# Norm factors by a power on GpSimd, a second norm from the first's statistics, and sigmoids as tanh, in a four-layer kernel on one core

## The chip, the cores and the metric

The chip is a Trainium2. The kernel runs on one of its cores, with that core's five engines: TensorE (PE; its weight loads are listed apart as PEld), VectorE (DVE), ScalarE (ACT), GpSimd (POOL) and SyncE (SP). Each engine works through its own queue of instructions in order, and waits on semaphores for the others. The metric is the device time of one launch in microseconds; the figure quoted for a kernel is the median of its runs.

## The reference, cut to what matters

Four batches of 1024 tokens with 128 features in float32, pass through four layers. Every layer has the same frame: a normalisation over the features, and then the sum of the input, an attention branch and a feed-forward branch, both fed with the normalised input.

```python
xn = _layernorm(x, axis=-1)          # (x - m) / sqrt(v + 1e-5), no gain, no bias
x = x + attn_l(xn, ...) + ffn_l(xn, ...)
```

Layer 0 has a memory attention and a mixture of eight experts, of which each token takes two. Layer 1 has a linear attention and a gated feed-forward with dequantised weights. Layer 2 is the one that the change touches most. Its attention branch normalises `xn` a second time, mixes neighbouring tokens by a convolution of width 3, and runs a gated recurrence over the tokens:

```python
h = (x - mu) * rsqrt(var + eps) * ln_g + ln_b       # x here is xn: a norm of a norm
mixed = conv_width_3(h) + mix_b
u, x_state = tanh(mixed @ Wi + bi), tanh(mixed @ Wsin + bsin)
decay, select = sigmoid(mixed @ Wd + bd), sigmoid(mixed @ Wsel + bsel)
state = decay * state + (1 - decay) * x_state       # scan over the tokens
y = (select * states) @ Wso + bso
g = sigmoid(mixed @ Wg + bg)
return x + (g * y + (1 - g) * u) @ Wout + bout
```

Layer 3 has an attention by phases (cosines and sines of learned angles), with a normalisation of what it retrieves, and a gated feed-forward in a 4-bit format.

## The kernel before, in words

The tokens of a batch lie on the 128 partitions in NT = 8 tiles of 128 features; B = 4 batches. `x[b]` (the running sum) and `xn[b]` (its norm) are 128x1024 tiles that stay in SBUF, and `xnT[b]` is `xn[b]` transposed, features on the partitions, with a zero column at either end.

`layernorm` (L198 to L213) takes one batch: eight `bn_stats` (L203) and eight `bn_aggr` (L205) on VectorE give mean and variance of the eight tiles as columns of `ln_mv`; ScalarE takes the square root of variance plus epsilon, eight columns at once (L207); VectorE takes its reciprocal (L208) and then does eight times subtract-and-multiply, 128x128 each (L210). ScalarE evaluates its functions from tables, and where the next function is in none that is loaded, an instruction ACT_TABLE_LOAD stands ahead of it, which the profile lists under the line of that function.

`prologue` (L230) runs `layernorm` from `x[b]` to `xn[b]` for its batches, and then `to_features` (L215), which transposes on TensorE (L220) and copies from PSUM on ScalarE (L223, or L225 with gain and bias). `add_psum` (L240) adds a PSUM result to half a batch of `x` on VectorE. `add_row` (L242) runs on GpSimd: it adds `xn` to `x` where asked (L245) and a row of biases to it (L246), each 128x1024.

The order of the stages is that of the Python; the order of instructions within each engine's queue is fixed when the kernel is built, by a scheduler that ranks what is ready, so work of later batches and of the next stage is interleaved with what goes before. At run time nothing overtakes. Queues that matter here are GpSimd's, VectorE's and ScalarE's.

Layer 0 ends with the experts: GpSimd scatters normalised tokens into lists by 64 indirect DMAs (L399), and the experts' results are gathered back by 64 more (L636), sixteen for each batch, in `combine` (L630), which layer 1 calls one batch ahead: the loop of layer 1 runs, for each batch, `attention(b)` (L648), the first half of `ffn`, `combine(b + 1)` and `prologue([b + 1])`, the second half of `ffn`, and `add_row`. The gathers have 24 buffers.

Layer 2 (L715 to L771) calls `prologue()` for all batches, then for each batch `layernorm(xn[b], hn)`, `add_row`, `to_features` into `hT` and the convolution on VectorE into `mixT` (L728 to L731). Then three projections of all batches into 128 partitions (32 states of 4 batches) give `xs`, `dec` and `sel` (L744), `drive`, and one scan of 1024 steps. In the loop over eight half batches after it, `u`, `g` and `y` are formed (L757 to L766) and projected into `po2`. `ffn` with Silu (L257) closes it.

Layer 3 (L775 to L945) calls `prologue()` and `add_row` for all batches, forms gates, and then goes batch by batch through the phases: sums in PSUM, products with cosines and sines on VectorE, GpSimd's running sums `run` (L887) and `rsum` (L894), `layernorm(bld, bld)` in place (L898), and the 4-bit feed-forward with Silu (L926), whose dequantised products `xq` and `hh` GpSimd forms (L294).

Of the kernel before, what the change touches and what calls it, by code (L numbers as in the profile page):

```python
# [10 lines left out]
F32 = mybir.dt.float32  # L11
I32 = mybir.dt.int32
AF = mybir.ActivationFunctionType
ALU = mybir.AluOpType
AX = mybir.AxisListType

P = 128
D = 128
B = 4
L = 1024  # L20
NT = L // P
NTT = B * NT
TB = 512
# [13 lines left out]
LN_EPS = 1e-5  # L37
# [32 lines left out]
def _cut(t, cols):  # L70
    out, at = {}, 0
    for name, n in cols:
        out[name] = t[:, at : at + n]
        at += n
    return out
# [3 lines left out]
def decoder4_kernel(  # L79
# [21 lines left out]
    V, S, G, T = nc.vector, nc.scalar, nc.gpsimd, nc.tensor  # L101

    const = ctx.enter_context(tc.tile_pool(name="const", bufs=1))
    state = ctx.enter_context(tc.tile_pool(name="state", bufs=1))
    small = ctx.enter_context(tc.tile_pool(name="small", bufs=2))
# [12 lines left out]
    def ps(name="ps"):  # L118
        n_ps[0] += 1
        return psum.tile([P, 512], F32, tag="ps", name=f"{name}_{n_ps[0]}")  # L120

    def pf(name):
        n_ps[0] += 1
        return psum.tile([P, 512], F32, tag="pf", name=f"{name}_{n_ps[0]}")


    x = []
# [28 lines left out]
    eps_c = const.tile([P, 1], F32, tag="eps", name="eps_c")  # L156
# [9 lines left out]
    W2 = _cut(w2_sb, W2_COLS)  # L166
# [19 lines left out]
    xn = [state.tile([P, NT, D], F32, tag=f"xn{b}", name=f"xn{b}") for b in range(B)]  # L186

    xnT = [state.tile([P, L + 2], F32, tag=f"xnT{b}", name=f"xnT{b}") for b in range(B)]
# [4 lines left out]
    def blk(t, i):  # L193

        c = 1 + (i % 2) * TB
        return t[i // 2][:, c : c + TB]

    def layernorm(src, dst):  # L198

        st = small.tile([P, NT, 6], F32, tag="ln_st", name="ln_st")  # L200
        mv = small.tile([P, NT, 2], F32, tag="ln_mv", name="ln_mv")
        for j in range(NT):
            V.bn_stats(st[:, j, :], src[:, j, :])  # L203
        for j in range(NT):
            V.bn_aggr(mv[:, j, :], st[:, j, :])  # L205
        rstd = small.tile([P, NT], F32, tag="ln_rstd", name="ln_rstd")
        S.activation(rstd, mv[:, :, 1], AF.Sqrt, bias=eps_c)  # L207
        V.reciprocal(rstd, rstd)  # L208
        for j in range(NT):
            V.tensor_scalar(  # L210
                dst[:, j, :], src[:, j, :], mv[:, j, 0:1], rstd[:, j : j + 1],
                ALU.subtract, ALU.mult,
            )  # L213

    def to_features(src, dst, g=None, bias=None):  # L215

        for h in range(2):
            pt = ps("pt")
            for j in range(4):
                T.transpose(pt[:, j * P : (j + 1) * P], src[:, 4 * h + j, :], ident)  # L220
            cols = dst[:, 1 + h * TB : 1 + (h + 1) * TB]
            if g is None:
                S.copy(cols, pt)  # L223
            else:
                S.activation(cols, pt, AF.Identity, bias=bias, scale=g)  # L225

    def mm(o, lhsT, rhs, start=True, stop=True):
        T.matmul(o, lhsT, rhs, start=start, stop=stop)  # L228

    def prologue(batches=range(B)):  # L230
        for b in batches:
            layernorm(x[b], xn[b])
        for b in batches:
            to_features(xn[b], xnT[b])

    def add_psum(i, p):

        h = (i % 2) * 4
        xv = x[i // 2][:, h : h + 4, :].rearrange("p j d -> p (j d)")
        V.tensor_tensor(xv, p, xv, ALU.add)  # L240

    def add_row(b, row, also=None):  # L242

        if also is not None:
            G.tensor_tensor(x[b], x[b], also, ALU.add)  # L245
        G.tensor_tensor(x[b], x[b], row.unsqueeze(1).to_broadcast([P, NT, D]), ALU.add)  # L246

    def ffn(guf, dnf, pool, blocks=range(NBLK)):
        for i in blocks:
            xT = blk(xnT, i)  # L250
            hid = pool.tile([P, NHC, TB], F32, tag="ffn_hid", name="ffn_hid")
            for c in range(NHC):
                pg, pu = pf("pg"), pf("pu")
                mm(pg, guf[:, 0, c, :], xT)
                mm(pu, guf[:, 1, c, :], xT)
                sg = pool.tile([P, TB], F32, tag="ffn_sg", name="ffn_sg")
                S.activation(sg, pg, AF.Silu)  # L257
                V.tensor_tensor(hid[:, c, :], sg, pu, ALU.mult)  # L258
            po = pf("po")
            for j in range(4):  # L260
                for c in range(NHC):
                    mm(po[:, j * D : (j + 1) * D], hid[:, c, j * P : (j + 1) * P], dnf[:, c, :],
                       c == 0, c == NHC - 1)
            add_psum(i, po)
# [36 lines left out]
    for t in range(NTT):  # L301
        b, j = divmod(t, NT)
# [3 lines left out]
    def l0t(tag, n=NS):  # L306
        return l0w.tile([P, n], F32, tag=tag, name=tag)
# [13 lines left out]
    for n in range(2):  # L321
        m = l0t(f"m{n}", NTT)
        V.tensor_reduce(m, by_e(sc), AX.X, ALU.max)
        w = l0t("w")
# [71 lines left out]
    for t in range(NTT):  # L396
        b, j = divmod(t, NT)
# [155 lines left out]
    xsT, hT, ex, hid, po = {}, {}, {}, {}, {}  # L553
# [159 lines left out]


    with tc.tile_pool(name="l2p", bufs=2) as l2p, tc.tile_pool(name="l2s", bufs=1) as l2s:  # L715
        prologue()
        hT, mixT = [], []
        for b in range(B):
            hn = l2p.tile([P, NT, D], F32, tag="hn", name="hn")
            layernorm(xn[b], hn)  # L720
            add_row(b, R["bout2"], xn[b])
            h = big.tile([P, L + 2], F32, tag="b1", name="hT")
            G.memset(h[:, 0:1], 0.0)
            G.memset(h[:, L + 1 : L + 2], 0.0)
            to_features(hn, h, g=W2["ln_g"], bias=W2["ln_b"])
            mx = big.tile([P, L + 2], F32, tag="b2", name="mixT")
            mv = mx[:, 1 : L + 1]
            V.tensor_scalar(mv, h[:, 1 : L + 1], W2["mix_w"][:, 1:2], W2["mix_b"],  # L728
                            ALU.mult, ALU.add)
            V.scalar_tensor_tensor(mv, h[:, 0:L], W2["mix_w"][:, 0:1], mv, ALU.mult, ALU.add)  # L730
            V.scalar_tensor_tensor(mv, h[:, 2 : L + 2], W2["mix_w"][:, 2:3], mv,  # L731
                                   ALU.mult, ALU.add)
            hT.append(h)
            mixT.append(mx)

        par = {}
        for nm, w, bias, fn in (("xs", "Wsin", "bsin", AF.Tanh), ("dec", "Wd", "bd", AF.Sigmoid),
                                ("sel", "Wsel", "bsel", AF.Sigmoid)):
            t = l2s.tile([P, L], F32, tag=nm, name=nm)
            for h in range(2):  # L740
                pst = ps("pst")
                for b in range(B):
                    mm(pst[b * SD : (b + 1) * SD, :], W2[w], blk(mixT, 2 * b + h))
                S.activation(t[:, h * TB : (h + 1) * TB], pst, fn, bias=W2[bias])  # L744
            par[nm] = t
        drive = l2s.tile([P, L], F32, tag="drive", name="drive")
        V.scalar_tensor_tensor(drive, par["dec"], 1.0, par["xs"], ALU.subtract, ALU.mult)
        states = l2s.tile([P, L], F32, tag="states", name="states")
        V.tensor_tensor_scan(states, par["dec"], drive, 0.0, ALU.mult, ALU.subtract)
        V.tensor_tensor(states, par["sel"], states, ALU.mult)  # L750
        for i in range(NBLK):
            b, h = divmod(i, 2)
            mT = blk(mixT, i)
            pu, pgg, py = ps("pu2"), ps("pgg"), ps("py")
            mm(pu, W2["Wi"], mT)
            u = l2p.tile([P, TB], F32, tag="u", name="u")
            S.activation(u, pu, AF.Tanh, bias=W2["bi"])  # L757
            mm(pgg, W2["Wg"], mT)
            g = l2p.tile([P, TB], F32, tag="g", name="g")
            S.activation(g, pgg, AF.Sigmoid, bias=W2["bg"])  # L760
            rb = slice(b * SD, (b + 1) * SD)
            mm(py, W2["Wso"][rb, :], states[rb, h * TB : (h + 1) * TB])
            y = l2p.tile([P, TB], F32, tag="y", name="y")
            V.scalar_tensor_tensor(y, py, W2["bso"], u, ALU.add, ALU.subtract)
            V.tensor_tensor(y, y, g, ALU.mult)
            V.tensor_tensor(y, y, u, ALU.add)  # L766
            po = pf("po2")
            for j in range(4):
                mm(po[:, j * D : (j + 1) * D], y[:, j * P : (j + 1) * P], W2["Wout"])
            add_psum(i, po)  # L770
        ffn(*ffn_w[1], l2p)  # L771
    l12.close()
# [2 lines left out]
    with tc.tile_pool(name="l3s", bufs=1) as l3s:  # L775
# [61 lines left out]
        with (  # L837
# [5 lines left out]
            for b in range(B):  # L843
# [16 lines left out]
                for j in range(NT):  # L860
                    t = b * NT + j
# [39 lines left out]
                for h in range(2):  # L901
                    po = ps("po3")
# [6 lines left out]
                for h in range(2):  # L909
# [26 lines left out]
                    po = pf("pof")  # L936
# [99 lines left out]
```

## Time and profile before

| what | value |
|---|---|
| time, median of 3 runs (lowest to highest) | 1124.07 us (1120.93 to 1126.26) |
| the profiled execution's own time | 1128.6 us |
| its span | 1126.8 us |
| TensorE clock granted, mean | 0.83 |
| busy, PE / PEld / DVE / ACT / POOL | 779.8 / 528.4 / 619.7 / 347.6 / 278.6 us |
| square roots on ScalarE, and table loads ahead of them | 24 of 300 ns, and 15 of 1283 ns |
| POOL's scatters (L399) and gathers (L636) | 64 of 1045 ns, 64 of 967 ns |

Times in the profile are microseconds from the start of the span. A row of a group gives engine and operation, output and input by name, shapes, the count, then busy time and the mean of one in ns, then how long the engine had been idle just before and what released it. A row of the timeline gives the start, the length, the engine, the line and the operation, and in brackets the idle time before it with its releaser; "issue" is a wait for nothing that the profile shows, and "remote" one for an event that it can't place. The profiled execution is one of its own and lies 4.5 us above the median.

### The profile page before, as it was taken

What the parts mean: (1) busy time and instruction counts of PE and PEld (TensorE: products, weight loads), DVE (VectorE), ACT (ScalarE), POOL (GpSimd) and SP (SyncE); (2) the same over time, 40 slices, a digit from 0 to 9 for tenths busy, and PEclk for the clock granted to TensorE, in tenths of its full rate; (3) what the DMA queues carried; (4) which work ended last, traced back from release to release, by engine and by line L of the source; (5) the groups of instructions that cost most, each with busy time, mean ns of one, the idle gap of its engine ahead of it and who ended that gap; (6) DMA issues with size and microseconds to landing.
All of it is one profiled execution on the core that took longest, in us unless ns stands there. A gap on an engine that the chain in (4) does not pass through costs nothing.

```text
span 1126.8 us, 10401 instructions
## 1 busy us (share of the span) xinstructions
PE 779.8 (69%) x3432; PEld 528.4 (47%) x3432; DVE 619.7 (55%) x1644; ACT 347.6 (31%) x551; POOL 278.6 (25%) x276
## 2 busy tenths in 40 slices
PE   2685156899991564695826999889967676667763
PEld 1543133566660243463612456555745555446652
DVE  6493023344443245659786546640187796796773
ACT  2041012233330252564624224421332314214121
POOL 2067720000005706112230003120032231341420
PEclk9988677999996777988957799967697797788867
DMA  9511100022211101000000000000000000000000
GB/s 341 160 36 49 52 23 16 29 76 68 73 55 51 54 6 37 10 10 1 1 1 0 1 1 1 1 0 1 1 0 1 10 10 10 10 0 10 10 3 16
DMA packets 44090, 34.73 MB, mean 31 GB/s; under 512 B 3334, under 2 KB 41030, under 8 KB 43782
## 3 DMA queue, kind: packets, MB, share of 16 engines
q1 hardware_dynamic: 39414, 23.61, 6.9%
q0 software_dynamic: 4624, 10.46, 3.0%
q8 instruction: 28, 0.46, 0.2%
q14 instruction: 24, 0.20, 0.1%
HBM read 18.40 MB, written 15.66 MB: 30 GB/s over the span
## 4 chain that ended last, share of the span: by engine, by line
PE 50%; DVE 22%; ACT 8%; another core or an unknown queue 7%; issue 6%; POOL 5%; DMA 1%; POOLq 0%; SPq 0%; ACTq 0%; DVEq 0%
PE ph L228 6%; PE po L228 5%; PE pg L228 4%; PE pu L228 4%; PE pm L228 3%; PE plg L228 3%; PE pt L220 3%; PE pmoe L228 3%; PE pgh L228 2%; PE pof L228 2%; DVE ln_st L203 2%; PE pth L934 1%; POOL rsum L894 1%; DVE xn L210 1%
## 5 line engine op out<-in xcount | busy, mean ns | idle before, releaser
L399 POOL DMA_INDIRECT xs_d<-xn,slot x64 | 66.9, 1045 | 71.9 <-DVE slot L382 52.7
L636 POOL DMA_INDIRECT yg<-ys_d,slot x64 | 61.9, 967 | 69.6 <-DVE x L699 50.4
L228 PE MATMUL ph<-w_sb,xsT 128*128 x142 | 74.8, 610 | 4.5 <-ACT xsT L566 4.4
L220 PE MATMUL pt<-ident,xn 128*128 128x128 f32 x128 | 30.4, 382 | 62.1 <-DVE xn L210 34.3
L228 PE MATMUL po<-dnf,ffn_hid 128*128 128x128 f32 x384 | 54.4, 290 | 22.2 <-DVE ffn_hid L258 22.2
L228 PEld LDWEIGHTS po<-dnf,ffn_hid 128*128 128x128 f32 x384 | 52.0, 205 | 34.5 <-DVE ffn_hid L258 29.2
L228 PE MATMUL pu<-xnT,guf 128*128 128x512 f32 x96 | 52.4, 628 | 11.8 <-ACT ffn_sg L257 11.8
L228 PE MATMUL pm<-val,tri 128*128 128x256 f32 x64 | 25.4, 484 | 48.7 <-DVE val L870 43.7
L585 DVE COPY moe_hT<-ph 128x256 f32<-128x256 f32 x71 | 30.2, 425 | 50.4 <-PE ph L583 50.4
L228 PE MATMUL pg<-xnT,guf 128*128 128x512 f32 x96 | 54.5, 652 | 3.2 <-ACT ffn_sg L257 3.2
L894 POOL TENSOR_TENSOR rsum<-ret 128x256 f32<-128x256 f32 x32 | 27.3, 854 | 111.0 <-DVE ret L892 106.3
L220 PEld LDWEIGHTS pt<-ident,xn 128*128 128x128 f32 x128 | 21.3, 176 | 68.8 <-issue 29.8
L934 PE MATMUL pth<-ident,hh 128*128 128x128 f32 (+1 forms) x96 | 22.5, 395 | 39.9 <-POOL hh L294 39.9
L240 DVE TENSOR_TENSOR x<-po,x 128x512 f32<-128x512 f32 x32 | 22.0, 688 | 50.3 <-PE po L228 37.1
L258 DVE TENSOR_TENSOR ffn_hid<-ffn_sg,pu 128x512 f32<-128x512 f32 x48 | 32.8, 683 | 30.0 <-PE pu L228 15.6
L576 ACT ACTIVATE moe_sg<-ph 128x256 f32<-128x256 f32 x71 | 27.3, 385 | 64.1 <-PE ph L228 64.1
L257 ACT ACTIVATE ffn_sg<-pg 128x512 f32<-128x512 f32 x48 | 28.7, 597 | 57.6 <-PE pg L228 57.4
L228 PE MATMUL pmoe<-w3e_sb,moe_hT 128*128 x284 | 43.5, 276 | 0.6 <-DVE moe_hT L585 0.5
L228 PEld LDWEIGHTS pmoe<-w3e_sb,moe_hT 128*128 128x128 f32 x284 | 38.6, 191 | 9.1 <-issue 8.1
L578 DVE TENSOR_TENSOR moe_hid<-moe_sg,ph 128x256 f32<-128x256 f32 x71 | 29.3, 413 | 24.7 <-ACT moe_sg L576 24.7
L245 POOL TENSOR_TENSOR x<-x,xn 128x1024 f32<-128x1024 f32 x8 | 18.9, 2364 | 95.9 <-DVE xn L210 95.9
L246 POOL TENSOR_TENSOR x<-x,rows_sb 128x1024 f32<-128x1024 f32 x12 | 29.3, 2442 | 44.0 <-DVE x L240 43.5
(351 smaller groups left out, 1922.7 us busy)
## 6 DMA issues: line engine op xcount, KB each, us to landing
xs_d<-zeros SPq DMA_DIRECT2D x18, 256.0 KB, 4.5
xs<-xs_d SPq DMA_DIRECT2D x17, 256.0 KB, 2.8
ys_d<-ys SPq DMA_DIRECT2D x17, 256.0 KB, 2.3
x<-in_x_in_dram SPq DMA_DIRECT2D x4, 512.0 KB, 12.0
w_sb<-in_w12T_dram SPq DMA_DIRECT2D x1, 2048.0 KB, 15.9
out_dram<-x SPq DMA_DIRECT2D x8, 256.0 KB, 2.3
w3e_sb<-in_w3T_dram SPq DMA_DIRECT2D x1, 1024.0 KB
xs_d<-xn,slot POOLq DMA_INDIRECT x64
```

The source lines that it names most:

```text
L220: T.transpose(pt[:, j * P : (j + 1) * P], src[:, 4 * h + j, :], ident)
L228: T.matmul(o, lhsT, rhs, start=start, stop=stop)
L246: G.tensor_tensor(x[b], x[b], row.unsqueeze(1).to_broadcast([P, NT, D]), ALU.add)
L257: S.activation(sg, pg, AF.Silu)
L258: V.tensor_tensor(hid[:, c, :], sg, pu, ALU.mult)
L399: G.indirect_dma_start(out=views[2 * t + n], out_offset=bass.IndirectOffsetOnAxis(ap=slots[n][:, t : t + 1], axis=0), in_=xn[b][:, j, :], ...
L576: S.activation(sg, ph[:, :HM], AF.Silu)
L578: V.tensor_tensor(hid[k], sg, ph[:, HM:], ALU.mult)
L585: V.tensor_copy(hT[k].rearrange("p c s -> p (c s)"), ph2[:, : 2 * P])
L636: G.indirect_dma_start(out=yg, out_offset=None, in_=ys_d, in_offset=bass.IndirectOffsetOnAxis(ap=slots[n][:, t : t + 1], axis=0),)
L894: G.tensor_tensor(rsum, ret[:, :, 0, :], ret[:, :, 1, :], ALU.add)
L934: T.transpose(pt[:n, j * P : (j + 1) * P], hh[:, j, o : o + n], ident)
```

## The change

It has three parts.

- The norm's factor: ScalarE's square root and VectorE's reciprocal are replaced by a multiply-and-add of eight columns on VectorE (variance plus epsilon) and a power of -1/2 on GpSimd (`rsqrt`). A constant tile `half_n` holds the exponent.
- In layer 2 the second norm is no longer measured. The first norm's output has mean 0, and its variance is known from the first's: rstd squared times the variance. `layernorm` gets an argument `again` for this; eight more multiplications, 128x128 each, write `hn`. The call of `prologue()` gives way to `layernorm` and `to_features` inside the loop over batches.
- In layer 2 the sigmoids become tanh of half the argument: sigmoid(z) = (tanh(z/2) + 1)/2. The halves go into biases (`hb`), into ScalarE's scale, and into scaled weights (`Wso4`, `Wout2`); `dec` needs one more multiply-and-add on VectorE, and three tensor-by-tensor instructions become ones that take a scalar too.

```diff
@@ -195,7 +195,16 @@
         c = 1 + (i % 2) * TB
         return t[i // 2][:, c : c + TB]
 
-    def layernorm(src, dst):
+    half_n = const.tile([P, NT], F32, tag="half_n", name="half_n")
+    G.memset(half_n, -0.5)
+
+    def rsqrt(dst, src, scale=1.0):
+
+        V.tensor_scalar(dst, src, scale, LN_EPS, ALU.mult, ALU.add)
+        G.tensor_tensor(dst, dst, half_n, ALU.pow)
+
+    def layernorm(src, dst, again=None):
+
 
         st = small.tile([P, NT, 6], F32, tag="ln_st", name="ln_st")
         mv = small.tile([P, NT, 2], F32, tag="ln_mv", name="ln_mv")
@@ -204,13 +213,19 @@
         for j in range(NT):
             V.bn_aggr(mv[:, j, :], st[:, j, :])
         rstd = small.tile([P, NT], F32, tag="ln_rstd", name="ln_rstd")
-        S.activation(rstd, mv[:, :, 1], AF.Sqrt, bias=eps_c)
-        V.reciprocal(rstd, rstd)
+        rsqrt(rstd, mv[:, :, 1])
         for j in range(NT):
             V.tensor_scalar(
                 dst[:, j, :], src[:, j, :], mv[:, j, 0:1], rstd[:, j : j + 1],
                 ALU.subtract, ALU.mult,
             )
+        if again is not None:
+            r2 = small.tile([P, NT], F32, tag="ln_r2", name="ln_r2")
+            V.tensor_tensor(r2, rstd, rstd, ALU.mult)
+            V.tensor_tensor(r2, r2, mv[:, :, 1], ALU.mult)
+            rsqrt(r2, r2)
+            for j in range(NT):
+                V.tensor_scalar(again[:, j, :], dst[:, j, :], r2[:, j : j + 1], None, ALU.mult)
 
     def to_features(src, dst, g=None, bias=None):
 
@@ -713,11 +728,19 @@
 
 
     with tc.tile_pool(name="l2p", bufs=2) as l2p, tc.tile_pool(name="l2s", bufs=1) as l2s:
-        prologue()
+
+        Wso4 = l2s.tile([P, D], F32, tag="Wso4", name="Wso4")
+        V.tensor_scalar(Wso4, W2["Wso"], 0.25, None, ALU.mult)
+        Wout2 = l2s.tile([P, D], F32, tag="Wout2", name="Wout2")
+        V.tensor_scalar(Wout2, W2["Wout"], 0.5, None, ALU.mult)
+        hb = l2s.tile([P, 3], F32, tag="hb", name="hb")
+        for n, nm in enumerate(("bd", "bsel", "bg")):
+            V.tensor_scalar(hb[:, n : n + 1], W2[nm], 0.5, None, ALU.mult)
         hT, mixT = [], []
         for b in range(B):
             hn = l2p.tile([P, NT, D], F32, tag="hn", name="hn")
-            layernorm(xn[b], hn)
+            layernorm(x[b], xn[b], hn)
+            to_features(xn[b], xnT[b])
             add_row(b, R["bout2"], xn[b])
             h = big.tile([P, L + 2], F32, tag="b1", name="hT")
             G.memset(h[:, 0:1], 0.0)
@@ -734,20 +757,22 @@
             mixT.append(mx)
 
         par = {}
-        for nm, w, bias, fn in (("xs", "Wsin", "bsin", AF.Tanh), ("dec", "Wd", "bd", AF.Sigmoid),
-                                ("sel", "Wsel", "bsel", AF.Sigmoid)):
+        for nm, w, bias, scale in (("xs", "Wsin", W2["bsin"], 1.0), ("dec", "Wd", hb[:, 0:1], 0.5),
+                                   ("sel", "Wsel", hb[:, 1:2], 0.5)):
             t = l2s.tile([P, L], F32, tag=nm, name=nm)
             for h in range(2):
                 pst = ps("pst")
                 for b in range(B):
                     mm(pst[b * SD : (b + 1) * SD, :], W2[w], blk(mixT, 2 * b + h))
-                S.activation(t[:, h * TB : (h + 1) * TB], pst, fn, bias=W2[bias])
+                S.activation(t[:, h * TB : (h + 1) * TB], pst, AF.Tanh, bias=bias, scale=scale)
             par[nm] = t
+
         drive = l2s.tile([P, L], F32, tag="drive", name="drive")
         V.scalar_tensor_tensor(drive, par["dec"], 1.0, par["xs"], ALU.subtract, ALU.mult)
+        V.tensor_scalar(par["dec"], par["dec"], 0.5, 0.5, ALU.mult, ALU.add)
         states = l2s.tile([P, L], F32, tag="states", name="states")
         V.tensor_tensor_scan(states, par["dec"], drive, 0.0, ALU.mult, ALU.subtract)
-        V.tensor_tensor(states, par["sel"], states, ALU.mult)
+        V.scalar_tensor_tensor(states, par["sel"], 1.0, states, ALU.add, ALU.mult)
         for i in range(NBLK):
             b, h = divmod(i, 2)
             mT = blk(mixT, i)
@@ -757,16 +782,17 @@
             S.activation(u, pu, AF.Tanh, bias=W2["bi"])
             mm(pgg, W2["Wg"], mT)
             g = l2p.tile([P, TB], F32, tag="g", name="g")
-            S.activation(g, pgg, AF.Sigmoid, bias=W2["bg"])
+            S.activation(g, pgg, AF.Tanh, bias=hb[:, 2:3], scale=0.5)
             rb = slice(b * SD, (b + 1) * SD)
-            mm(py, W2["Wso"][rb, :], states[rb, h * TB : (h + 1) * TB])
+            mm(py, Wso4[rb, :], states[rb, h * TB : (h + 1) * TB])
+
             y = l2p.tile([P, TB], F32, tag="y", name="y")
             V.scalar_tensor_tensor(y, py, W2["bso"], u, ALU.add, ALU.subtract)
-            V.tensor_tensor(y, y, g, ALU.mult)
-            V.tensor_tensor(y, y, u, ALU.add)
+            V.scalar_tensor_tensor(y, g, 1.0, y, ALU.add, ALU.mult)
+            V.scalar_tensor_tensor(y, u, 2.0, y, ALU.mult, ALU.add)
             po = pf("po2")
             for j in range(4):
-                mm(po[:, j * D : (j + 1) * D], y[:, j * P : (j + 1) * P], W2["Wout"])
+                mm(po[:, j * D : (j + 1) * D], y[:, j * P : (j + 1) * P], Wout2)
             add_psum(i, po)
         ffn(*ffn_w[1], l2p)
     l12.close()
```

## The prediction

> **What bounds the kernel now.** First the page: busy shares and the chain that ended last.
>
> ```profile
> PE 779.8 (69%) x3432; PEld 528.4 (47%) x3432; DVE 619.7 (55%) x1644; ACT 347.6 (31%) x551; POOL 278.6 (25%) x276
> PE 50%; DVE 22%; ACT 8%; another core or an unknown queue 7%; issue 6%; POOL 5%; DMA 1%; POOLq 0%; SPq 0%; ACTq 0%; DVEq 0%
> ```
>
> No engine bounds the whole, and ACT, which the change relieves most, holds 8% of the chain. So second, busy time by stretch (columns: stretch: length, then busy us and count of PE, PEld, DVE, ACT, POOL, then clock and DMA). I cut at the stages' ends: 345 to 446 is layer 1 while POOL gathers, 562 to 607 is layer 2's head, 607 to 664 its scan and mix, 812 to 1127 layer 3's batches.
>
> ```profile
> 345.00:446.00 101.00, 40.71 (x151) 26.10 (x151) 35.41 (x127) 24.20 (x35) 53.66 (x59) 0.70 0.13 37
> 562.00:607.00 45.00, 15.67 (x64) 8.55 (x63) 38.68 (x139) 11.46 (x19) 11.66 (x5) 0.58 0.00 1
> 607.00:664.00 57.00, 51.46 (x160) 22.21 (x160) 28.22 (x38) 20.43 (x28) 0.17 (x3) 0.85 0.00 0
> 812.00:1127.00 315.00, 207.39 (x974) 165.27 (x972) 228.86 (x491) 88.63 (x135) 87.19 (x69) 0.81 0.03 7
> ```
>
> Layer 2's head is VectorE's alone (38.7 of 45 us). From 607 PE rules; layer 3's batches are shared; in the gathers nobody is busy. Third, VectorE's groups inside 562 to 607:
>
> ```profile
> L210 DVE TENSOR_SCALAR hn<-xn,ln_mv,ln_rstd 128x128 f32<-128x128 f32 x32 | 12.1, 451 | 0.0
> L203 DVE BATCH_NORM_STATS2 ln_st<-xn 128x6 f32<-128x128 f32 x32 | 6.9, 273 | 0.0
> L205 DVE BATCH_NORM_AGGREGATE ln_mv<-ln_st 128x2 f32<-128x6 f32 x40 | 4.0, 155 | 0.0
> L208 DVE RECIPROCAL ln_rstd<-ln_rstd 128x8 f32<-128x8 f32 x5 | 0.9, 187 | 0.0
> ```
>
> The second norm's statistics, all 32 of them, stand here. Fourth, ACT's groups, whose last column says what the square roots and their loads wait for:
>
> ```profile
> L207 ACT ACT_TABLE_LOAD x15 | 19.2, 1283 | 7.2 <-DVE ln_mv L205 7.0
> L744 ACT ACT_TABLE_LOAD x2 | 2.6, 1283 | 4.8 <-PE pst L228 4.7
> L207 ACT ACTIVATE ln_rstd<-ln_mv,eps_c 128x8 f32<-128x8 f32 x24 | 7.0, 300 | 89.8 <-DVE ln_mv L205 65.1 <-DVE x L640 24.6
> ```
>
> ACT stood idle 89.8 us ahead of the square roots: it had loaded and was waiting. Most loads are therefore hidden. Fifth, POOL, since the power goes there: its timeline in the gathers, and two rows of its groups.
>
> ```profile
> 440.52 0.95 POOL L636 DMA_INDIRECT yg<-ys_d,slot  x1 [0.30 <-issue]
> 441.77 0.95 POOL L636 DMA_INDIRECT yg<-ys_d,slot  x1 [0.30 <-issue]
> ```
>
> ```profile
> L894 POOL TENSOR_TENSOR rsum<-ret 128x256 f32<-128x256 f32 x32 | 27.3, 854 | 111.0 <-DVE ret L892 106.3 <-DVE ln_mv L205 4.7
> L887 POOL TENSOR_TENSOR run<-run,val 128x512 f32<-128x512 f32 x20 | 26.6, 1328 | 28.0 <-DVE val L872 26.2 <-DVE ln_st L203 1.8
> ```
>
> Gathers follow each other every 1.25 us, in order; whatever is built behind them waits.
>
> **What the Trainium skill says.** "ScalarE: Activation LUTs", section "What ACT_TABLE_LOAD costs", gives about 1283 ns for a load and a drain behind it; the trace has 1283 ns for each and shows ACT's next activation starting at once (load at 1097.74, Silu at 1099.03), so I price a load at 1.28. "GPSIMD Engine Reference", sections 1 and 2.1: its SBUF port is shared with VectorE. The trace agrees: eight normalisations take 2.14 us alone, and 5.65 beside POOL's adds at 574.16. The same page, section 7, gives an fp32 dependent chain 4 cycles an element; no page prices a power.
>
> **The power's price.** The trace has none. Lower end, from the two POOL rows: (1328-854)/256 = 1.85 ns a column, so 380 ns at zero width and 0.4 us at 8 columns. Upper end: if it is a chain of 50 steps of 4 cycles at 1.2 GHz, 0.17 us a column, 1.3 us, plus 0.4: an estimate of 1.7 from that page; lane by lane it could be over 10. I take P = 0.6. It replaces a square root (0.30) and a reciprocal (0.20) by a VectorE scale-and-add (0.1) and the power, with two hand-overs as before: nothing at P = 0.4, +0.2 here, some 12 times on the path: two in layer 0, four in layer 1, two in layer 2, four in layer 3. That is +2.5 in all; it is within the stage sums below.
>
> **Part by part.** The build order of the changed kernel has 26 fewer table loads (33.4 us of ACT) and 24 fewer square roots (7.0 us).
>
> *Layer 0:* the first load is issued at 7.0 while x still lands (until 15.6), and VectorE has the statistics of other batches to do between a root and its use: 0 (-1 to +2; with a power of 2 us or more its cover is gone, and the excess counts twice).
>
> *Layer 1, a loss.* The powers stand in POOL's order after gathers 22, 55 and 64. Batch 0: square root at 368.35; gather 22 ends at 373.1, so +5. PE then runs into a stall it has anyway: from 377 to 404 it got 'remote' or 'issue' waits of 9 to 10 us, ending only when the gathers ended (395.7, last release 401.6). I take +2 (1 to 5.5). Batch 1: square root at 429.33, gather 55 ends at 441.5, +12; VectorE stands behind it, but its next instruction, the residual add L240, was released only at 445.30, as was ACT's qz. The transposes and xnT then finish after that instead of before, so pq is late by about 2.7 (1 to 6). Batch 2: square root 478.76, gather 64 ends at 482.63, normalisation at 479.44 becomes 483.3; the residual add waited for PE until 485.5, so pq at 485.30 slips to about 488: +3 (2 to 4). Batch 3 has no gathers: 0. Sum +7.5 (4 to 15).
>
> *Layer 2's head, the gain.* Now 44.0 us, from the end of layer 1's last residual add at 562.85 to that of the last mixT at 606.82. Removed on VectorE: 6.9 + 32 x 0.155 less overlap, 3.2, + 4 x 0.19 = 10.9 us. Added: two 8-column products and two scale-and-adds per batch, most before 562, about 0.8 in here; two 128x128 weight scalings and three tiny bias ones, 0.6. Batches 1 to 3 also lose waits between their second statistics and hn, but batch 3 gains a serial step: POOL's add L245 (2.35 us) sits ahead of its second power, so VectorE waits some 2 us where it now has mixT work to do. Normalisations beside POOL's adds are stretched either way (3.5 us now at 574). Net -9 (-12 to -5). The SP queue moves nowhere.
>
> *Sigmoids.* At L744 tanh stands between loads at 608 and 610.65: 2.6 us, with PE's products done and VectorE waiting for dec and sel, so on the path: -2.6; the new dec scale-and-add of 128x1024 (nearest row L728, 0.81 us, on a narrower mix of operands) lands between drive and scan: +0.7. Net -1.9. The y chain has the same three VectorE instructions.
>
> *Rest of layer 2 and layer 3's head (664 to 812).* PE is busy 66 of 71 and 73 of 77 us. Four Sqrt-Silu pairs go; each delayed a Silu by 1.3 to 2.6, of which PE noticed 0.3 to 1: -2.5 (-4 to -1).
>
> *Layer 3's batches.* Four Sqrt loads, all hidden (ACT idle 3.5 to 9.4 us before the root), and four Silu loads go (sine and Silu share a set in the build). The last, at 1097.74, delays Silu by about 0.4 as the product ends at 1098.6; the one at 866.40 by 1.3. The power in batch 1 waits behind hh on POOL (937.43, 2.59 us) but PE waited for that hh until 940.07. -2 (-5 to +3).
>
> Sum: 7.5 - 9 - 1.9 - 2.5 - 2 = -7.9, against the profiled execution, 1128.6 us (span 1126.8 and 1.8 around it): 1120.7. That one lies 4.5 above the median 1124.07, so the same step gives 1116.
>
> **Rivals.** Bound of what can be told: 0.5%, 5.6 us.
> *A, a dear power (slower).* The sum turns at P = 0.6 + 7.9/12 = 1.26 us, and is 0.5% slower from 1.7. At 3 us: -7.9 + 12 x 2.4 = +21, 1145. For it: a power is a long loop in software, unpriced. Against: 8 columns only. Chance 0.17.
> *B, the gathers' queue uncovered.* If PE's stalls move along with the late norms, layer 1 pays 5 + 12 + 4 = 21: 1129.6. For it: PE waited 27.6 us for that first root. Against: the stalls end with the gathers, which start no later. 0.13.
> *C, layer 1 absorbs it all* and VectorE's whole 12 us in the head count: 0 - 12 - 1.9 - 4 - 2 = -20, 1104. For it: the stall ends are POOL's. 0.17.
> *D, nothing seen*: the head's gain is given back by POOL's serial adds (5 us) and layer 1: 1122 to 1126. 0.08.
>
> **The numbers.** Forecast case 0.45, its own range 1109 to 1122: 0.38 of it is below 1118.4, 0.07 within. Faster 0.38 + 0.17 = 0.55; same 0.07 + half of B, 0.06, + 0.08 = 0.21; slower 0.07 + 0.17 = 0.24. Range: from just under C, 1102, up through B into A, 1135 (P about 2.2), leaving some 0.18.
>
> **What would show it.** Right: 44 table loads; POOL rows of 128x8 under 0.8 us; mixT's last instruction about 35 us after layer 1's last residual add instead of 44; norms of batches 0 and 1 in layer 1 starting right behind a gather, at about 374 and 442, and Silu of layer 1 only 2 to 3 us late each time. Wrong: powers above 1.3 us; gathers held up by a power that waits; a head that still ends after 44 us, with VectorE waiting for POOL.

## The result

The changed kernel is slower: 1130.51 us (median of 9 runs, 1127.08 to 1135.92) against 1122.91 us (9 runs, 1118.21 to 1127.67), a ratio of 1.0072 with an interval of 1.0044 to 1.0101. The forecast was 1116 and faster. The time lies in the range given, on the wrong side. Here and below a median is over all runs of a kernel, while a ratio leaves out the executions that ran in a slower, disturbed state.

The two profiled executions don't show that loss: 1128.6 us before is above all nine runs of before, and 1127.08 us after is the lowest of after. So I cut both executions into stages and ask, for each, whether other kernels with the same code in that stage repeat its length. First the page of the changed kernel, busy shares and chain:

```profile
PE 765.5 (68%) x3432; PEld 518.0 (46%) x3432; DVE 618.9 (55%) x1594; ACT 308.1 (27%) x501; POOL 322.5 (29%) x301
PE 48%; DVE 24%; issue 8%; ACT 6%; POOL 6%; another core or an unknown queue 5%; DMA 1%; POOLq 0%; SPq 0%; ACTq 0%; DVEq 0%
```

ScalarE is relieved of 39.5 us and GpSimd loaded with 43.9; nothing of that says where the end moved. The groups give the reason for the second number (columns as before: busy us, mean ns of one, idle before it):

```profile
L204 POOL TENSOR_TENSOR ln_rstd<-ln_rstd,half_n 128x8 f32<-128x8 f32 x20 | 33.0, 1650 | 107.0 <-DVE ln_rstd L203 106.9
L204 POOL TENSOR_TENSOR ln_r<-ln_r,half_n 128x8 f32<-128x8 f32 x4 | 6.6, 1647 | 11.1 <-DVE ln_r L203 11.0
```

A power of eight columns takes 1.65 us. The stages, in us, read from the start or end of the instruction named:

| stage, up to | before | after | difference |
|---|---|---|---|
| first scatter | 60.5 | 61.8 | +1.3 |
| end of the experts | 282.0 | 276.7 | -5.3 |
| (to the first gather) | 3.3 | 3.3 | 0 |
| layer 1's last residual add | 217.1 | 233.5 | +16.4 |
| layer 2's last mixT | 44.0 | 39.0 | -5.0 |
| layer 2's second residual add | 28.1 | 22.0 | -6.1 |
| layer 2's last residual add | 91.5 | 90.2 | -1.3 |
| the copy of layer 3's gate logits | 83.9 | 74.6 | -9.4 |
| the last residual add | 312.9 | 320.9 | +8.0 |

The experts' -5.3 is not explained. No norm stands in that stretch, and four other kernels that take every root on ScalarE up to there took 278.8 to 284.0 for it; but the changed kernel and two others with the power ahead of it took 276.5 to 276.7, a third 280.1, so it need not be chance. Layer 1 of before varies too: those four, which have its norms as before has them, took 211.8, 213.6, 213.9 and 217.4 us for it, so 217.1 is at the long end. And most of the -6.1 in front of the second residual add of layer 2 is TensorE's clock, as the experiments show below. A stage of one pair of traces is good to some 4 or 5 us, where nothing else repeats it.

The windows of three stages, before and after (columns: stretch: length, then busy us and count of PE, PEld, DVE, ACT, POOL, then clock, DMA). Before:

```profile
345.74:562.84 217.10, 130.74 (x564) 88.75 (x564) 121.48 (x419) 92.14 (x130) 79.54 (x72) 0.80 0.07 20
726.47:810.40 83.93, 75.46 (x253) 47.99 (x254) 19.70 (x48) 17.80 (x26) 9.44 (x7) 0.69 0.00 0
810.40:1123.32 312.92, 208.99 (x976) 166.12 (x975) 230.46 (x496) 90.17 (x136) 87.19 (x69) 0.81 0.02 6
```

After:

```profile
341.81:575.36 233.55, 132.40 (x548) 88.47 (x548) 123.81 (x426) 81.37 (x113) 99.01 (x82) 0.77 0.07 18
726.48:801.03 74.55, 71.44 (x267) 45.87 (x266) 20.12 (x48) 19.78 (x30) 10.59 (x8) 0.74 0.00 1
801.03:1121.89 320.86, 204.38 (x976) 161.44 (x975) 234.40 (x495) 78.81 (x124) 93.50 (x73) 0.81 0.02 6
```

In layer 1 VectorE and PE have nearly the same work as before and 16 us more to do it in: the time is waiting. VectorE's timeline of batch 1, and GpSimd's beside it:

```profile
425.54 0.66 DVE L273 TENSOR_TENSOR ffn_hid<-ffn_sg,pu 128x512 f32<-128x512 f32 x1
426.11 0.17 DVE L203 TENSOR_SCALAR ln_rstd<-ln_mv 128x8 f32<-128x8 f32 x1
440.07 1.25 DVE L218 TENSOR_SCALAR xn<-x,ln_mv,ln_rstd 128x128 f32<-128x128 f32 x4 [13.79 <-issue]
```

```profile
436.12 0.95 POOL L651 DMA_INDIRECT yg<-ys_d,slot  x1 [0.30 <-issue]
437.38 0.96 POOL L651 DMA_INDIRECT yg<-ys_d,slot  x1 [0.31 <-issue]
438.37 1.67 POOL L204 TENSOR_TENSOR ln_rstd<-ln_rstd,half_n 128x8 f32<-128x8 f32 x1
440.23 1.07 POOL L651 DMA_INDIRECT yg<-ys_d,slot  x1 [0.19 <-issue]
```

The variance is ready at 426.28. The power stands behind gathers that have nothing to do with it until 438.37, and VectorE does nothing for 13.79 us. From the end of VectorE's scale-and-add (L203) to the first normalisation (L218) the four batches wait 6.45, 13.79, 4.92 and 1.83 us, 27.0 in all. Before, from the end of the square root to the same instruction, it was 0.27, 0.39, 0.38 and 1.58. In batch 1 of before the root ends at 429.63, and the normalisation follows the reciprocal at once; the next residual add, though, came late in any case:

```profile
430.01 2.14 DVE L210 TENSOR_SCALAR xn<-x,ln_mv,ln_rstd 128x128 f32<-128x128 f32 x8
445.30 0.69 DVE L240 TENSOR_TENSOR x<-po,x 128x512 f32<-128x512 f32 x1 [13.15 <-remote]
```

The same add in the changed kernel:

```profile
445.29 0.69 DVE L255 TENSOR_TENSOR x<-po,x 128x512 f32<-128x512 f32 x1 [3.08 <-PE po L243]
```

Counted from the first gather, the residual adds that follow the norms of batches 1, 2 and 3 start at 99.6, 139.8 and 178.6 us before, and at 103.5, 150.2 and 192.2 in the changed kernel. So of the 16.4 us that layer 1 is longer, 3.9 are there behind batch 1's norm, 10.4 behind batch 2's and 13.6 behind batch 3's.

### The profile page after: what moved, and what is told of

Read it like the earlier page. It is cut to its first block, busy times and chain, and to the rows that moved or that the text cites. A ratio compares the mean times of both kernels' runs of the same rounds, so it can differ in the third digit from the quotient of the medians.

```text
span 1125.3 us, 10313 instructions
## 1 busy us (share of the span) xinstructions
PE 765.5 (68%) x3432; PEld 518.0 (46%) x3432; DVE 618.9 (55%) x1594; ACT 308.1 (27%) x501; POOL 322.5 (29%) x301
## 4 chain that ended last, share of the span: by engine, by line
PE 48%; DVE 24%; issue 8%; ACT 6%; POOL 6%; another core or an unknown queue 5%; DMA 1%; POOLq 0%; SPq 0%; ACTq 0%; DVEq 0%
PE ph L243 6%; PE po L243 5%; PE pu L243 4%; PE pm L243 4%; PE pg L243 4%; PE plg L243 3%; PE pmoe L243 3%; DVE xn L218 2%; PE pgh L243 2%; PE pt L235 2%; POOL ln_rstd L204 2%; PE pof L243 2%; POOL yg L651 2%; POOL rsum L920 2%
## 5 line engine op out<-in xcount | busy, mean ns | idle before, releaser
L414 POOL DMA_INDIRECT xs_d<-xn,slot x64 | 71.5, 1117 | 52.5 <-DVE slot L397 33.3
L243 PE MATMUL po<-dnf,ffn_hid 128*128 128x128 f32 x384 | 59.1, 306 | 25.1 <-DVE ffn_hid L273 25.1
L243 PEld LDWEIGHTS po<-dnf,ffn_hid 128*128 128x128 f32 x384 | 56.0, 220 | 39.3 <-DVE ffn_hid L273 34.0
L204 POOL TENSOR_TENSOR ln_rstd<-ln_rstd,half_n 128x8 f32<-128x8 f32 x20 | 33.0, 1650 | 107.0 <-DVE ln_rstd L203 106.9
L235 PEld LDWEIGHTS pt<-ident,xn 128*128 128x128 f32 x128 | 20.6, 172 | 91.8 <-issue 66.5
L218 DVE TENSOR_SCALAR xn<-x,ln_mv,ln_rstd 128x128 f32<-128x128 f32 x128 | 37.5, 363 | 38.2 <-issue 20.2
L238 ACT COPY xnT<-pt 128x512 f32<-128x512 f32 x32 | 18.2, 591 | 141.4 <-PE pt L235 140.7
```

What stands on the lines that cost most here:

```text
L204: G.tensor_tensor(dst, dst, half_n, ALU.pow)
L218: V.tensor_scalar(dst[:, j, :], src[:, j, :], mv[:, j, 0:1], rstd[:, j : j + 1], ALU.subtract, ALU.mult,)
L414: G.indirect_dma_start(out=views[2 * t + n], out_offset=bass.IndirectOffsetOnAxis(ap=slots[n][:, t : t + 1], axis=0), in_=xn[b][:, j, :], ...
```

## The experiments

My theory T is that the power is the whole loss, by its price and by what it stands behind, and that the other two parts gain. Rival R: the power is nearly paid for by the loads saved, and the second norm's new order costs. The runs come from several chips, so each is judged by its ratio to the kernel before on its own chip.

**The three parts alone, and two without the third.** The power alone (in the kernel before, with `rsqrt` and `half_n` as in the change):

```diff
-        S.activation(rstd, mv[:, :, 1], AF.Sqrt, bias=eps_c)
-        V.reciprocal(rstd, rstd)
+        rsqrt(rstd, mv[:, :, 1])
```

> The kernel before with the power in place of square root and reciprocal, and nothing else of the change: 24 norms, the second of layer 2 still measured. Theory T (the power is the whole loss: 1.65 us apiece, queued behind gathers and adds, and VectorE stands behind it): slower than before by 14 to 20 us, that is more than the whole change, with 2 of the three parts giving some back. Rival R (the power is nearly paid for by the loads it saves, and the second norm's new order in layer 2 costs): slower by 3 us at most.

The second norm alone, both factors by root and reciprocal:

```diff
-        prologue()
...
-            layernorm(xn[b], hn)
+            layernorm(x[b], xn[b], hn)
+            to_features(xn[b], xnT[b])
```

> The kernel before with layer 2's second norm from the first's statistics, both factors by square root and reciprocal as before, sigmoids kept. T: faster by 6 to 10 us, layer 2's head ending some 7 to 9 us after layer 1's last residual add earlier than before. R: 0 to 8 us slower, the loss sitting at the end of layer 1 and in layer 2's head, where GpSimd's add now stands ahead of what VectorE needs.

The tanh alone, that is the change's last part with `prologue()` and the norms left as before:

```diff
-                S.activation(t[:, h * TB : (h + 1) * TB], pst, fn, bias=W2[bias])
+                S.activation(t[:, h * TB : (h + 1) * TB], pst, AF.Tanh, bias=bias, scale=scale)
...
+        V.tensor_scalar(par["dec"], par["dec"], 0.5, 0.5, ALU.mult, ALU.add)
```

> The kernel before with the sigmoids as tanh and nothing else. T and R alike: two table loads fewer after the head, one multiply-and-add more: 1 to 3 us faster, at the edge of what can be told.

Everything but the power:

```diff
-        V.tensor_scalar(dst, src, scale, LN_EPS, ALU.mult, ALU.add)
-        G.tensor_tensor(dst, dst, half_n, ALU.pow)
+        S.activation(dst, src, AF.Sqrt, bias=eps_c)
+        V.reciprocal(dst, dst)
```

> The whole change but for the power: second norm from the first's statistics and tanh, both factors by square root and reciprocal on ScalarE and VectorE. T: 8 to 12 us faster than before, and so 16 to 20 faster than the changed kernel. R: within 4 us of the changed kernel.

| kernel | median us | ratio to before, 95% |
|---|---|---|
| power alone | 1147.82 | 1.024 (1.0187 to 1.0293) |
| second norm alone | 1119.12 | 0.992 (0.9881 to 0.9959) |
| tanh alone | 1125.76 | 0.9937 (0.9883 to 0.9991) |
| both, no power | 1116.48 | 0.9912 (0.9883 to 0.9942) |
| before, same chip | 1125.49 | |

R falls: the power alone loses more than the whole change does, and without it the change gains 0.9%, about 10 us. T expected 14 to 20 us for the power; it was 2.4%, 27 us by the ratio and 22 at the medians. The tanh alone can't be told from nothing: its ratio is just under 1, its median is that of before.

The second norm gains 4.4 us where it was looked for: from layer 1's last residual add to the last mixT 39.6 us instead of 44.0. From there to the second residual add it takes 23.2 instead of 28.1, and the tanh alone 25.9; but that is not work saved. The stretch falls into two at the end of `states` (the scan and the product after it). Before, the second norm alone, and then the same code in layer 2 twice (the run with layer 3's inner norms on the root, and the changed kernel run again, both further below):

```profile
618.12:634.94 16.82, 16.77 (x34) 7.12 (x34) 6.91 (x11) 3.02 (x5) 0.00 (x0) 0.59 0.00 1
607.68:619.59 11.91, 11.85 (x34) 5.05 (x34) 6.83 (x12) 3.02 (x5) 0.00 (x0) 0.86 0.01 1
624.16:639.35 15.19, 15.13 (x34) 6.61 (x34) 6.92 (x12) 3.03 (x5) 0.00 (x0) 0.66 0.00 1
586.79:597.05 10.26, 10.21 (x34) 4.69 (x34) 6.82 (x11) 3.03 (x5) 0.00 (x0) 1.00 0.01 2
```

Up to the end of `states` before and the second norm alone take 11.30 us each, the tanh alone 10.75, the changed kernel 10.05. Behind it 34 matmuls of PE take 10.3 to 16.8 us, the lower the granted clock the longer (0.59, 0.66, 0.86, 1.00), and with the same code as well. So of the second norm's 9.3 us in its two stretches 4.9 came with the clock, of the tanh's 2.2 some 1.6, and of the changed kernel's -6.1 all but 1.25. With the second norm not measured and roots in layer 2 this part took 11.9 us in four kernels and 13.4 in a fifth, in three that measure it 15.2 to 16.8; that the new second norm brings the better clock is therefore likely, but why is not shown.

**Layer 1's four norms back on the root**, the other 20 powers kept. A flag that is set ahead of each group of norms selects the way; this run, and three more below, differ only in where it is set:

```diff
     def rsqrt(dst, src, scale=1.0):
+        if by_root[0]:
+            S.activation(dst, src, AF.Sqrt, bias=eps_c)
+            V.reciprocal(dst, dst)
+            return
...
+        by_root[0] = True
         combine(0)
```

> The changed kernel with layer 1's four norms back on square root and reciprocal; the other 20 powers stay. T (the gathers' queue on GpSimd is the dearest place of the power): 14 to 20 us faster than the changed kernel, some 1112 to 1117, and batch 1's first residual add in layer 1 no longer tied to the end of the gathers. Rival U (every power costs alike, about 1 us of its 1.65): 4 to 5 us faster than the changed kernel.

1124.93 us, ratio 0.9973 (0.9944 to 1.0001): about 1% less than the changed kernel's 1.0072, and in the trace layer 1 takes 221.5 us instead of 233.5. So 12 us, between the two expectations: dearer than U, less than T's 14. Up to batch 3 its residual adds stand where those of before do (99.5, 139.9 and 180.0 us after the first gather, against 99.6, 139.8 and 178.6), the late one of batch 1 included. At the end of layer 1 it is 4.4 us later than before: layer 2's first powers stand in layer 1's tail. With these the pair's 16.4 is accounted for, 12.0 for layer 1's own powers and 4.4 for layer 2's.

**Every power run twice**, the first into a spare tile:

```diff
+        twice = small.tile([P, NT], F32, tag="twice", name="twice")
+        G.tensor_tensor(twice, dst, half_n, ALU.pow)
         G.tensor_tensor(dst, dst, half_n, ALU.pow)
```

> The changed kernel with each power run twice, the first into a spare tile: 1.65 us of GpSimd more before each factor. If the power is on the path in about 14 places (four in layer 1, four in layer 2, two in layer 3's head, four in its batches): 20 to 26 us slower than the changed kernel. If the trouble is the queue in front of the power and not its own length: 10 us slower or less.

1174.2 us, ratio 1.0399 (1.0352 to 1.0445), so 3.3% or some 37 us over the changed kernel's ratio and 43.7 at the medians. The 24 powers added are worth 24 x 1.65 = 39.6. I had counted 14 places on the path; in sum the added powers cost as if all 24 stood on it. Layer 2's feed-forward, which hid its four powers (90.2 us against 91.5), does not hide eight (100.1). Where one power fits into a wait, two don't.

**Layer 3's four inner norms back on the root** (the flag set ahead of `layernorm(bld, bld)`):

> The changed kernel with only the four norms inside layer 3's batches back on square root and reciprocal. T: the stretch from layer 3's head to the end takes 6 to 10 us less than in the changed kernel, whole time as much. U: 4 us less. If the loads that come back cost what the power did: no difference.

1120.83 us, ratio 1.0008 (0.9975 to 1.004), some 7 us under the changed kernel's ratio; the stretch from the gate logits to the end takes 308.8 us instead of 320.9. T holds, in the trace at 12 us above its 6 to 10. VectorE's waits in that stretch of the changed kernel say half of why (columns: waited for, us in total, times, longest):

```profile
DVE bld L921 <- POOL rsum L920: 11.4, 18, 0.9
DVE bld L218 <- POOL ln_rstd L204: 7.0, 4, 1.8
```

Before had in that stretch:

```profile
DVE ln_rstd L208 <- ACT ln_rstd L207: 1.1, 3, 0.4
```

Four waits of 1.75 us stand where the root cost 1.1 in all, which is 5.9 of the 12 us. For the rest there is a rival, the order of the queues: the instructions of VectorE and of ScalarE in these batches have one order in all kernels that keep the root here, and another in all that don't. The kernel without any root, below, has the changed kernel's order and no power to wait for, and takes 313.5 us; four kernels with powers here take 320.8 to 321.0, eight with roots 307.0 to 312.9. So the powers cost some 7.3 us, as their waits of 7.0 say, and the removal of roots and loads gained nothing; what is left of the 12 lies with the order, or within the 6 us over which the kernels with roots differ.

**The power in layer 3's first norms alone**, roots elsewhere. In both kernels with powers everywhere layer 3's head had become 9 us shorter, which nothing in my theory asked for:

> Second norm from the first's statistics and tanh, every factor by square root and reciprocal but the four of layer 3's first norm, which keep the power. If the 9 us that layer 3's head was shorter by in both kernels with the power come from it: 6 to 9 us faster than the same kernel without any power (that one was 1116 at the median), with the head at 75 us and not 84. If they come from an earlier stage or from the clock: as long as that one, within 3 us.

1110.23 us, ratio 0.9843 (0.98 to 0.9886): the fastest of this study among those that take all their roots, 1.6% under before. Its head takes 77.5 us, 6.3 less than in the kernel with all roots and the rest of the change, and its batches 3.1 less. So the gain is that of layer 3's first norms. Whether it is the power or the absence of roots there, the last but one run of the next group tells.

**Other chips.** The next three ran on a chip, and the fourth on a further one, where the kernel before takes about 1070 us (1069.47 and 1071.34), so that times expected in absolute terms don't carry over; differences and stages do. Layer 1's powers alone, roots elsewhere:

> Second norm from the first's statistics and tanh, every factor by square root and reciprocal but the four of layer 1, which are powers on GpSimd. If layer 1's four powers by themselves cost what their queue says (waits of 5 to 14 us on VectorE, partly covered): 10 to 15 us slower than the same kernel without any power (1116 at the median), so 1126 to 1131. If their cost only came with layer 2's powers standing in the same queue: 5 us slower or less.

No root in any norm (it leaves the square root out):

```diff
-        G.tensor_tensor(dst, dst, half_n, ALU.pow)
+        V.reciprocal(dst, dst)
```

> The changed kernel with the power left out: the factor is the reciprocal of variance plus epsilon, on VectorE, so no root is taken at all, on any engine (this leaves out part of the norm). It is the floor of what any other place for the root could reach. If the rest of the change is worth 9 to 10 us, layer 3's head 6 to 9 and the free tables about 3: 1100 to 1106. If ScalarE's roots are as good as free outside layer 3's head: no faster than 1108.

The same in layer 3's first norms only, roots on ScalarE elsewhere:

> Roots on ScalarE everywhere but in layer 3's first norm, where no root is taken (reciprocal of variance plus epsilon on VectorE; this leaves out part of the norm). If layer 3's head is shorter because the square roots and their loads are gone from ScalarE: the head takes 73 to 78 us here as well, as with the power. If it is shorter because of where the power puts the work that follows it: 82 to 84 us.

And the changed kernel once more:

> The changed kernel as it is, a second time, to see how much of its loss in layer 1 depends on the stalls that cover the power's queue. If the stalls of TensorE while GpSimd issues its DMAs are there (scatters to experts' end 196 us, gathers' start to layer 1's last residual add 233 us): ratio near 1.007 again. If they are not (175 us and 208 us or less): layer 1 loses 20 us and more against the same stretch with roots, 187 us, and the ratio is 1.01 to 1.02.

| kernel | median us | ratio to before, 95% | layer 1 | layer 3's head |
|---|---|---|---|---|
| layer 1's powers alone | 1091.14 | 1.021 (1.0166 to 1.0254) | 210.1 | 83.9 |
| no root anywhere | 1050.91 | 0.9821 (0.9776 to 0.9866) | 189.1 | 76.4 |
| no root in layer 3's head | 1049.69 | 0.9815 (0.9777 to 0.9854) | 187.1 | 76.0 |
| the changed kernel | 1092.58 | 1.02 (1.0166 to 1.0235) | 214.7 | 74.5 |

Three things follow. First, on these chips the change loses 2%, some 21 us, and layer 1 loses more than that: 214.7 against 187.1 us with roots. Four powers cost 23 us there (210.1 against 187.1), against 10 to 15 expected and a sum of VectorE's waits of 25.4; nearly all of each wait is paid. Nor is it the changed order of the queues: the kernel without any root has the changed kernel's order on ScalarE and GpSimd in layer 1 and takes 189.1. The windows of layer 1, with roots and with powers:

```profile
317.01:504.06 187.05, 124.31 (x548) 86.20 (x548) 120.92 (x424) 91.93 (x129) 78.92 (x71) 0.84 0.09 23
```

```profile
322.32:537.05 214.73, 126.98 (x548) 85.41 (x548) 123.72 (x426) 81.05 (x113) 98.97 (x82) 0.77 0.08 20
```

And VectorE's batch 1 in the second of them, with the power that it waits for:

```profile
389.29 0.17 DVE L203 TENSOR_SCALAR ln_rstd<-ln_mv 128x8 f32<-128x8 f32 x1
403.19 0.92 DVE L218 TENSOR_SCALAR xn<-x,ln_mv,ln_rstd 128x128 f32<-128x128 f32 x3 [13.73 <-POOL ln_rstd L204]
```

```profile
401.48 1.68 POOL L204 TENSOR_TENSOR ln_rstd<-ln_rstd,half_n 128x8 f32<-128x8 f32 x1
```

The wait is the same to 0.1 us, 13.73 and 13.79, as on the first chip. What differs is the rest: on the first chips PE and ScalarE stall while GpSimd issues DMAs, as before's residual add at 445.30 does, and a wait that falls together with such a stall costs less. That this is what made the power cheaper there is argued from the comparison; no run switches the stalls off on one chip. Between gathers 40 and 41 lie 25.3 us in the changed kernel's first execution, 7.9 here; the stretch from the first scatter to the experts' end takes 257.2 instead of 276.7. The page's chain here no longer has the share of an unknown queue:

```profile
PE 46%; DVE 24%; POOL 14%; issue 8%; ACT 6%; DMA 2%; POOLq 0%; SPq 0%; DVEq 0%; ACTq 0%
```

Second, no root anywhere is in sum no faster than roots on ScalarE everywhere but in layer 3's head (0.9821 and 0.9815, each to within half a per cent). Stage by stage ScalarE's roots are not all free: layer 2's head takes 35.8 us without and 39.7 with them, but layer 3's batches, with their other order, 313.5 against 310.4, and layer 1 189.1 against 187.1. A cheaper place could gain some 4 us in layer 2's head, and nothing that these runs show elsewhere. Third, layer 3's head is short wherever the roots are off ScalarE's queue there, by a power or by nothing (74.5 to 77.5, one power each), and long where they are on it (82.5 to 83.9). Its ScalarE timelines show what moves. Before:

```profile
728.15 0.30 ACT L207 ACTIVATE ln_rstd<-ln_mv,eps_c 128x8 f32<-128x8 f32 x1 [3.18 <-DVE ln_mv L205]
...
739.90 0.63 ACT L287 ACTIVATE qx_v<-qx_m 128x512 f32<-128x512 f32 x1 [6.38 <-POOL xq L294]
740.55 1.28 ACT L792 ACT_TABLE_LOAD   x1
741.84 0.69 ACT L792 ACTIVATE ghT<-pgh,w_sb 128x512 f32<-128x512 f32 x1
```

After:

```profile
734.74 0.59 ACT L238 COPY xnT<-pt 128x512 f32<-128x512 f32 x1 [0.56 <-PE pt L235]
735.34 1.28 ACT L818 ACT_TABLE_LOAD   x1
736.64 0.69 ACT L818 ACTIVATE ghT<-pgh,w_sb 128x512 f32<-128x512 f32 x1
...
741.62 0.63 ACT L302 ACTIVATE qx_v<-qx_m 128x512 f32<-128x512 f32 x1 [2.41 <-POOL xq L309]
```

Before, the build put the second `qx_v` ahead of the first Gelu, and it waited 6.38 us for GpSimd's `xq`; with no root in the queue it put it behind, in this kernel and in those with no root in the head alone. The first Gelu starts 10.2 us after layer 2's last residual add instead of 15.4, which is 5.2 of the 9.4 us. The rest goes with a higher clock in that stretch (0.74 against 0.69) and is not taken apart further.

## Why the prediction was wrong, point by point

- **"I take P = 0.6."** It is 1.65, at the upper end of the bounds (0.4 to 1.7). The lower end came from rows of additions and said nothing of a power. With the prediction's own formula, -7.9 + 12 x (1.65 - 0.6) = +4.7, the forecast would have been 1129, against 1130.5: rival A, whose turning point of 1.26 us was passed. That agreement is luck in part, since the other terms were off and partly cancel. So is the upper bound's: the 50 steps behind it were assumed.
- **Layer 1, "+7.5 (4 to 15)".** It was +16.4 in the profiled pair, outside the range, and 20 against the kernel with roots and the rest of the change. The waits were read rightly (+5 and +12 forecast in front of batches 0 and 1; 6.2 and 13.4 more measured), and so was their place behind gathers 22, 55 and 64. In the pair the cover of batch 1 held as well: +2 and +2.7 were forecast up to there, and 3.9 came. What failed is what lies behind. Batch 2 added 6.5 instead of 3; batch 3, put at 0 because it has no gathers, added 3.2; and layer 2's first powers, which stand in layer 1's tail, were left out (4.4 here by the run with layer 1's roots; 214.7 against 210.1 on the other chips). The cover was also less certain than the forecast had it: with the norms of layer 1 as before, other executions had the residual add L240 end 15.0 (three times), 20.6 and 23.3 us after gather 41 began, against 23.3 in before, and against those with 15.0 batch 1 alone loses 12 us. On the chips where before takes 1070 us it ends 13.5 us after it, with roots. Rival B, 21 us "uncovered", describes these (23).
- **Layer 2's head, "-9".** The stage as the forecast defines it, up to the last mixT, gave 5.0 in the changed kernel, at the end of the range, and 4.4 in the run that has the second norm alone. In that run VectorE is busy there for 34.8 us instead of 37.8, where 10.9 were to go and 1.4 to come: the 32 multiplications for hn took 14.9 us instead of 12.1, two products of eight columns 2.5. The total of 9.3 that the run shows up to the second residual add fits the forecast only by way of PE's clock, which the forecast does not have.
- **Sigmoids, "-1.9".** The path was right and the size too large: 0.55 us up to the end of `states` in the run that has the tanh alone, which loses one of the two loads, and 1.25 in the changed kernel, which loses both.
- **Rest of layer 2 and layer 3's head, "-2.5".** Layer 2's feed-forward gave 1.3. The head gave 9.4, not foreseen. The step costed the removed loads alone and took the order of ScalarE's queue as given; it changes with the roots gone, `qx_v` with the first Gelu.
- **Layer 3's batches, "-2 (-5 to +3)".** +8.0, outside its range. The Silu loads removed were worth nothing that shows (313.5 us without roots and loads, 307.0 to 312.9 with them), and four waits of 1.75 us on VectorE, the engine that has the most to do there, replaced waits of 1.1 us in all. The forecast had put the power's own wait there at +0.2 each.
- **"Most loads are therefore hidden"** was right: with no root in any norm the sum is no better than with roots outside one stage, and layer 2's head alone shows a gain, of 3.9 us.

The stages, the experts left out, sum to 1.3 + 16.4 - 5.0 - 6.1 - 1.3 - 9.4 + 8.0 = +3.9, against +7.6 between the medians. With the experts' -5.3, the clock in the -6.1 and the long layer 1 of before, one pair can't be added up more closely than that. In the pair, layer 1 is off by +9, layer 2's feed-forward and layer 3's head by -8, layer 3's batches by +10. The step that failed first is the price of the power, put at 0.6 us and measured at 1.65. Beside it, batch 3 of layer 1, layer 2's first norms in its tail and the new order of the queues in layer 3 were put at nothing.

## What to carry to other kernels

An operation without a row and without a price decides a change when it stands 24 times in a dependent chain; if the sum turns sign inside its bounds, the forecast should too. A small instruction in front of which an engine waits costs its place in its queue before its price: here 1.65 us of work made VectorE wait 13.8 behind gathers that didn't concern it. And a cover that consists of another stall, seen in one execution, is no cover until other executions show it. The parts are worth taking apart: the power in layer 3's first norms alone, with roots elsewhere and the other two parts of the change, is 1.6% faster than before, where the whole change is slower.

## What the runs showed of the hardware that was not expected

- GpSimd's power of 128x8 takes 1627 to 1701 ns in all the runs; by the slope of its additions in the trace of before (854 ns for 256 columns, 1328 for 512), an addition of eight columns would take about 0.4 us, an estimate.
- The same 34 matmuls behind layer 2's scan took PE 10.2 us at a granted clock of 1.00, 11.9 at 0.86, 15.1 at 0.66 and 16.8 at 0.59; the first and the third of these are the same code. What sets the clock is not shown.
- Two kinds of chip: the kernel before takes about 1125 us on two of the chips used, and in the first comparison nearly as much (1122.91), and about 1070 on two others. From first scatter to the experts' end a profiled execution takes 277 to 284 us on the former and 257 to 263 on the latter, and between gathers 40 and 41 lie 17 to 27 us on the former and 3 to 9 on the latter. Why events reach PE and ScalarE late on the former while GpSimd issues its DMAs stays open; no run was made on it.
